# A graph network kernel: three count tables, searches in two steps, and the neighbour sums of both layers by seven block products

## The chip, the cores and the metric

The kernel runs on one core of a Trainium2 chip. The metric is the device time of one execution in microseconds (us), the median of three runs. A profiled execution gives a trace of every instruction; its span runs from the first instruction to the last, and the time of the run is a little longer than its span. The engines are PE (TensorE, matrix products), DVE (VectorE), ACT (ScalarE), POOL (GpSimd) and SP (SyncE, which here only issues transfers). Each of them works through its own list of instructions in order.

## What is computed

Two blocks follow one another on 384 nodes with 1024 features, in float32:

```
h = relu(layernorm(x));  x = x + L0(h)      # attention with an edge mask
h = relu(layernorm(x));  x = x + L1(h)      # relational graph convolutions

L0: q, k, v = h @ w.T + b, then q2, k2, v2 = (q, k, v) @ wi.T + bi      # 1024 x 1024 each
    mask[src, dst] = softplus(weight of the edge's type), the last edge of a cell wins
    out = softmax(q2 k2.T / 8 + mask) v2 @ wo.T + bo                    # 16 heads

L1: x = relu(h @ w_in + b_in)                                           # 1024 -> 768
    twice:
        counts[r, n] = edges of type r that end in node n
        agg[n] = sum over edges (r, src -> n) of (x @ W_r)[src] / counts[r, n]
        x = batchnorm(relu(agg + x @ root + bias) + x)                  # W_r = sum_b comp[r, b] basis[b]
    out = layernorm(x @ w_out + b_out)
```

There are 12672 edges, six edge types in L1 and four basis matrices.

## The kernel before

**Edges.** The kernel keeps no list of messages. It builds dense tables in device memory: four mask tables of 384 x 384 cells and two count tables of 384 x 6 x 384 cells (`mtab`, `atab`, lines 169 and 170). The edges come in 99 chunks of 128. For each chunk one indirect transfer of POOL writes mask values (`put_mask`, L261) and one adds counts (`put_count`, L266). [...]DVE first compares the edges of a chunk with each other (`find_cells`, L250): one comparison for the mask's cell, one for the mask's cell with the edge type. A piece has up to 12 chunks, so a search is a first half of 12 comparisons, preceded by a shift (`cells`, L241), and a second half of 12. Counts 0 to 10 go to table 0, the later ones to the two tables in turn. The first counts are interleaved with the mask puts; most of them follow after the last mask put. The tables are cleared beforehand by transfers of zeros on SP (`clear`, L271).

**The order of the edge work** is written out by hand. `edge_steps` is a generator with a body per step; the projections call `fill(1)` once per quarter of a weight matrix, which runs one step. Which step clears what, searches which piece and puts which rounds is listed there.

**Projections.** q2, k, k2 and v are computed by seven block products in place of eight (`multiply`, L377): DVE forms sums S of weight blocks (`output_sums`, L371) and sums T of input blocks (`node_sum`, L364), and adds parts of the result (L496, L502, L504).

**Attention** follows, then the output product (L615) and the input product of L1 (`ps_x`).

**The graph layers.** A relation's counts A[r] (128 partitions x 3 x 384) are loaded from both count tables: near the end of attention SP loads two relations from table 0 (L656), POOL loads the other four (L660) and adds table 1 to each (L658). `add_up` (L332, L333) sums A[r] over its three blocks on POOL; `share` sums that over the partitions by a matrix product with ones (`ps_cnt`, L338), takes the reciprocal on DVE (L340, L341) and has POOL scale A[r] (L342). `mix` combines the six scaled relations into four matrices At[b], one per basis matrix: r = 0 on ACT (L324), r = 1 to 5 on DVE (L326). The dictionary `between` names, by layer, basis and piece of it, after which products a share or a mix is emitted:

```python
        between = {(0, 1, 1): shares(0), (0, 1, 2): shares(1),
```

For each layer PE first computes H[b] = X basis[b] for four b (L846 and L840; again seven block products, with DVE sums L780, L787, L789, L795 and additions L853, L861, L863), then X root (L880), then adds the neighbours' sum, which is H[b] times At[b] over four b and three blocks of nodes. In layer 0 this is done directly: 72 products of 384 columns (L897). In layer 1 it is done in halves, with seven block products of 192 columns in place of eight (L947), sums of At (L953 to L957), sums of H (L969) and additions (L979) on DVE. After it each feature block is rectified, added to the layer's input and normalised (L902 to L918). Layer 1's matrices At are mixed anew during its products.

A float32 product appears in the trace as two matmul instructions.

Of the kernel before, what the change touches and what calls it, by code (L numbers as in the profile page):

```python
# [51 lines left out]
def gnn_kernel(ctx: ExitStack, tc: tile.TileContext, out, x, edges, chunks, cols, rows, small,  # L52
# [117 lines left out]
    atab = [tables.tile([ACELLS + P, 1], F32, name=f"atab{i}") for i in range(2)]  # L170
    keys_d = tables.tile([PAD, P], I32, name="keys_d")

    def edge_steps(ep, none, zero):
# [90 lines left out]
        def put_count():  # L264
            i, c = next(counts)
            nc.gpsimd.indirect_dma_start(atab[0 if i < 18 - DEALT else i % 2][:, :],  # L266
                                         bass.IndirectOffsetOnAxis(at[:, 1, c:c + 1], 0),
                                         count[:, 1, c:c + 1], None, compute_op=ALU.add)
# [20 lines left out]
        for find_more in rest:  # L289
            find_more()  # L290
        for step in range(2, 18):
            yield
            for i in {5: (0,), 6: (1,), 7: (2, 3), 8: (4, 5)}.get(step, (step - 4,) if 10 <= step < 16 else ()):
                clear(i // R, i % R)
            if step in (3, 6, 8, 10, 12, 14, 16):
                find_cells(max(3, step // 2 + 1))()
            for p in {8: (3,), 9: (4,), 10: (5,), 11: (6,), 16: (7, 8), 17: (9,)}.get(step, ()):
                put_rounds(p)
# [35 lines left out]

    def share(r):
# [6 lines left out]
        nc.gpsimd.tensor_tensor(A[:, r], A[:, r], rn[:, None, :].to_broadcast([P, NT, N]), ALU.mult)  # L342
        if r + 2 < R:
            add_up(r + 2)


    with ExitStack() as inner:
# [284 lines left out]
        for g in range(STEPS + 1):  # L632
# [14 lines left out]
            if f + 2 == STEPS:  # L647
# [7 lines left out]
                for r in range(2):  # L655
                    nc.sync.dma_start(A[:, r], tabs[0][r])  # L656
                for r in range(R):
                    nc.gpsimd.dma_start(A[:, r], tabs[1][r], accum_op=ALU.add)  # L658
                    if r + 2 < R:
                        nc.gpsimd.dma_start(A[:, r + 2], tabs[0][r + 2])  # L660
                    if 0 < r < 3:
                        add_up(r - 1)
# [103 lines left out]
    with tc.tile_pool(name="conv", bufs=1) as cp:  # L766
# [41 lines left out]
        def mixes(l, r, *bs):  # L808
            return lambda: mix(l, r, At, bs)

        between = {(0, 1, 1): shares(0), (0, 1, 2): shares(1),
                   (0, 2, 0): lambda: (mix(0, 0, At), share(2)), (0, 2, 1): mixes(0, 1, 0, 1), (0, 2, 2): mixes(0, 1, 2, 3),
                   (0, 2, 4): shares(3),
                   (0, 3, 0): mixes(0, 2, 0, 1), (0, 3, 1): lambda: (mix(0, 2, At, (2, 3)), share(4)),
                   (0, 3, 2): mixes(0, 3, 0, 1), (0, 3, 4): shares(5),
                   (0, 4, 0): mixes(0, 4, 0, 1), (0, 4, 1): mixes(0, 5, 0, 1), (0, 4, 2): mixes(0, 3, 2, 3),
                   (0, 4, 3): mixes(0, 4, 2, 3), (0, 4, 4): mixes(0, 5, 2, 3),
# [10 lines left out]
        for l in range(L):  # L828
# [49 lines left out]
            for k in range(KC):  # L878
                for o in range(KC):
                    nc.tensor.matmul(pr[o], w[k // 2][:, k % 2, o * P:(o + 1) * P], XT[:, k, :], start=(k == 0),  # L880
                                     stop=(k == KC - 1 and l == L - 1))
                if k == 0:
                    rest()
                go_between(l, B, k)
            if l + 1 < L:
                w = load_basis(l + 1, 0)
            else:

                room = late.tile([P, R * NT * N], F32, tag="A", name="room")
                rowsB = room[:, :3 * D].rearrange("p (j d) -> p j d", j=3)  # L890
                for j, r in enumerate((R_BOUT, R_LNG, R_LNB)):
                    nc.scalar.dma_start(rowsB[:, j, :], rows[r:r + 1, :].to_broadcast([P, D]))

            def add_neighbours(o, bs):
                for b in bs:
                    for n in range(NT):
                        nc.tensor.matmul(pr[o], H_[:, b, n, o * P:(o + 1) * P], At[:, b, n, :],  # L897
                                         start=False, stop=(b == B - 1 and n == NT - 1))
# [21 lines left out]
            def begin(o, func=AF.Identity):  # L920

                c = l * KC + o
                nc.scalar.activation(XN[:, o, :], pr[o], func, bias=cols_sb[:, CB + c:CB + c + 1])

            if l + 1 < L:
                for o in range(KC):
                    add_neighbours(o, (0, 1))
                for o in range(KC):
                    add_neighbours(o, (2, 3))
                    begin(o, AF.Relu)  # L930
                    normalise_layer(*measure(o))
                    if o == 2:
                        T = weight_sums(w)
            else:


                def h(o, i):

                    return H_.rearrange("p b n d -> p (b n) d")[:, i * 6:i * 6 + 6, o * P:(o + 1) * P]

                def q(i, j):

                    return At.rearrange("p b n d -> p (b n) d")[:, i * 6:i * 6 + 6, j * HN:(j + 1) * HN]

                def times(ps, x, y, start=False, stop=True):
                    for c in range(6):
                        nc.tensor.matmul(ps, x[:, c], y[:, c], start=start and c == 0, stop=stop and c == 5,  # L947
                                         skip_group_check=True)

                room2 = keep.tile([P, KD * N], F32, tag="hT", name="room2")  # L950
                T1, T2 = [room2[:, i * 1152:(i + 1) * 1152].rearrange("p (c d) -> p c d", c=6) for i in range(2)]
                T4 = keep.tile([P, 6, HN], F32, tag="mask8", name="T4")
                nc.vector.tensor_tensor(T1, q(0, 1), q(0, 0), ALU.subtract)  # L953
                nc.vector.tensor_tensor(T2, q(1, 1), T1, ALU.subtract)
                T3 = q(0, 1)
                nc.vector.tensor_tensor(T3, q(1, 1), q(0, 1), ALU.subtract)
                nc.vector.tensor_tensor(T4, q(1, 0), T2, ALU.subtract)  # L957
                spaces = [room2[:, 2304:]] + [room[:, 3 * D + i * 768:3 * D + (i + 1) * 768] for i in range(5)]
                spaces = [v.rearrange("p (c o) -> p c o", c=6) for v in spaces]

                def feature_sums(p):

                    s0, s1, s3 = spaces[p % 2 * 3:][:3]
                    o0, o1 = 2 * p, 2 * p + 1
                    S.append((s0, s1, h(o1, 0), s3))
                    for dst, x, y, op in ((s0, h(o1, 0), h(o1, 1), ALU.add), (s1, s0, h(o0, 0), ALU.subtract),
                                          (h(o1, 0), h(o0, 0), h(o1, 0), ALU.subtract),
                                          (s3, h(o0, 1), s1, ALU.subtract)):
                        nc.vector.tensor_tensor(dst, x, y, op)  # L969
                        yield  # L970

                S = []
                for _ in feature_sums(0):
                    pass
                pairs = KC // 2

                def take(o, j, ps):
                    dst = XN[:, o, j * HN:(j + 1) * HN]
                    nc.vector.tensor_tensor(dst, dst, ps, ALU.add)  # L979

                def rectify(o):
                    nc.scalar.activation(XN[:, o, :], XN[:, o, :], AF.Relu)
                    return o

                def first_of(p):
# [146 lines left out]
```

## Time and profile before

| | |
|---|---|
| median of three runs | 737.99 us (736.06 to 738.41) |
| profiled execution | 735.77 us, span 734.0 us |
| PE busy | 713.5 us, 97% of the span |
| DVE busy | 472.9 us, 64% |
| POOL busy | 323.3 us, 44% |
| ACT busy | 147.2 us, 20% |
| granted PE clock, mean | 0.996 of full |
| count puts, L266 | 99, 160.0 us busy, 1616 ns each |
| transfers A<-atab on POOL | 10 of 576 KB |

The page gives for each engine its busy time and share of the span. A row of a group reads: line, engine, operation, written<-read, shapes, number, then busy time, mean time of one, idle time of the engine before it and what ended that. A line of the waits view reads: engine, line that waited, what it waited for, us in total, times, longest. A line in order of time begins with its start and its length in us; in brackets stands the idle time before it and what released it. Matmuls overlap, so their pace is read from start to start.

### The profile page before, as it was taken

What the parts mean: (1) busy time and instruction counts of PE and PEld (TensorE: products, weight loads), DVE (VectorE), ACT (ScalarE), POOL (GpSimd) and SP (SyncE); (2) the same over time, 40 slices, a digit from 0 to 9 for tenths busy, and PEclk for the clock granted to TensorE, in tenths of its full rate; (3) what the DMA queues carried; (4) which work ended last, traced back from release to release, by engine and by line L of the source; (5) the groups of instructions that cost most, each with busy time, mean ns of one, the idle gap of its engine ahead of it and who ended that gap; (6) DMA issues with size and microseconds to landing.
All of it is one profiled execution on the core that took longest, in us unless ns stands there. A gap on an engine that the chain in (4) does not pass through costs nothing.

```text
span 734.0 us, 8299 instructions
## 1 busy us (share of the span) xinstructions
PE 713.5 (97%) x3024; PEld 496.8 (68%) x3024; DVE 472.9 (64%) x1228; ACT 147.2 (20%) x338; POOL 323.3 (44%) x242
## 2 busy tenths in 40 slices
PE   8999989999999999999999999899999999999995
PEld 8759989999964444445995555555555555579943
DVE  6895897877504499625424779990187676506756
ACT  3201111111111477510131131100013111001100
POOL 1456777788886788587784454310000000030000
PEclk9999999999999999999999999999999999999999
DMA  7797766743447322623527953321003123700001
GB/s 296 261 346 231 221 182 209 212 148 115 116 119 240 59 1 2 215 0 47 127 2 169 312 163 129 129 83 46 0 1 107 66 85 129 271 29 1 1 29 57
DMA packets 40533, 90.96 MB, mean 124 GB/s; under 512 B 19644, under 2 KB 27680, under 8 KB 36270
## 3 DMA queue, kind: packets, MB, share of 16 engines
q1 hardware_dynamic: 18478, 79.62, 30.9%
q0 software_dynamic: 21008, 8.42, 10.4%
q10 hardware_dynamic: 1008, 2.41, 0.9%
q8 instruction: 23, 0.38, 0.2%
q14 instruction: 16, 0.13, 0.1%
HBM read 79.27 MB, written 11.16 MB: 123 GB/s over the span
## 4 chain that ended last, share of the span: by engine, by line
PE 86%; DVE 11%; ACT 1%; issue 1%; DMA 1%; DVEq 0%; ACTq 0%
PE ps_g L846 13%; PE ps_g L840 10%; PE ps_c L897 6%; PE ps_c L880 6%; PE ps_q L395 6%; PE ps_v L524 6%; PE ps_k L377 6%; PE ps_c L947 6%; PE ps_v L377 5%; PE ps_y L615 5%; PE ps_f L1054 4%; DVE same L250 3%; PE ps_q L377 3%; PE ps_x L377 3%; PE ps_o L608 2%; PE ps_s L563 2%
## 5 line engine op out<-in xcount | busy, mean ns | idle before, releaser
L266 POOL DMA_INDIRECT atab<-count,at x99 | 160.0, 1616 | 50.6 <-DMA atab<-count,at 26.2
L261 POOL DMA_INDIRECT mtab<-m_val,at x99 | 104.1, 1052 | 57.0 <-issue 24.4
L1041 POOL TENSOR_TENSOR x_sb<-x_sb,room 128x1024 f32<-128x1024 f32 x3 | 7.0, 2347 | 158.1 <-DMA room<-in_rows 158.1
L326 DVE SCALAR_TENSOR_TENSOR At<-A,small_sb,At 128x1152 f32<-128x1152 f32 x40 | 62.9, 1635 | 0.0
L840 PE MATMUL ps_g<-T,S 128*128 128x384 f32 x144 | 49.1, 486 | 0.0
L846 PE MATMUL ps_g<-w_c,XT 128*128 128x384 f32 x144 | 48.0, 487 | 0.0
L846 PE MATMUL ps_g<-w_c,XN 128*128 128x384 f32 x144 | 47.6, 486 | 0.0
L897 PE MATMUL ps_c<-At,H 128*128 128x384 f32 x144 | 46.6, 486 | 0.0
L395 PE MATMUL ps_q<-hT,w_q 128*128 128x384 f32 (+1 forms) x160 | 41.8, 422 | 1.4 <-ACT hT L90 1.4
L524 PE MATMUL ps_v<-w_v,v 128*128 128x512 f32 x96 | 41.9, 594 | 0.0
L840 PEld LDWEIGHTS ps_g<-T,S 128*128 128x128 f32 x144 | 27.4, 190 | 19.1
L897 PEld LDWEIGHTS ps_c<-At,H 128*128 128x128 f32 x144 | 27.4, 190 | 19.1
L846 PEld LDWEIGHTS ps_g<-w_c,XN 128*128 128x128 f32 x144 | 27.4, 190 | 19.1
L846 PEld LDWEIGHTS ps_g<-w_c,XT 128*128 128x128 f32 x144 | 27.2, 190 | 19.2 <-DVE H L861 0.6
L395 PEld LDWEIGHTS ps_q<-hT,w_q 128*128 128x128 f32 x160 | 28.5, 190 | 14.1 <-ACT hT L90 1.7
L377 PE MATMUL ps_k<-T,S 128*128 128x192 f32 x192 | 35.8, 330 | 0.0
L615 PE MATMUL ps_y<-w_o,attT 128*128 128x512 f32 x80 | 35.0, 595 | 0.0
L576 DVE CUSTOM_DVE_ANT_0 s<-ps_s,mask 128x384 f32<-128x384 f32 x48 | 24.5, 548 | 15.4 <-PE ps_s L563 15.4
L342 POOL TENSOR_TENSOR A<-A,rn 128x1152 f32<-128x1152 f32 x6 | 19.4, 3236 | 31.7 <-DVE rn L341 31.7
L524 PEld LDWEIGHTS ps_v<-w_v,v 128*128 128x128 f32 x96 | 18.0, 190 | 22.6 <-issue 22.6
L377 PEld LDWEIGHTS ps_k<-T,S 128*128 128x128 f32 x192 | 32.7, 194 | 0.0
L1054 PE MATMUL ps_f<-w_out,XN 128*128 128x512 f32 (+1 forms) x84 | 31.1, 531 | 0.0
(250 smaller groups left out, 1316.6 us busy)
## 6 DMA issues: line engine op xcount, KB each, us to landing
w_c<-in_basis SPq DMA_DIRECT2D x24, 768.0 KB, 6.2
atab<-zero SPq DMA_DIRECT2D x12, 576.0 KB, 8.2
A<-atab POOLq DMA_DIRECT2D x10, 576.0 KB, 9.8
w_c<-in_root SPq DMA_DIRECT2D x6, 768.0 KB, 5.5
w_q<-in_wq SPq DMA_DIRECT2D x4, 1024.0 KB, 11.8
w_q<-in_wiq SPq DMA_DIRECT2D x4, 1024.0 KB, 10.1
w_k<-in_wk SPq DMA_DIRECT2D x4, 1024.0 KB, 7.0
w_k<-in_wik SPq DMA_DIRECT2D x4, 1024.0 KB, 6.2
```

The lines of the kernel that those rows point to most:

```text
L261: nc.gpsimd.indirect_dma_start(mtab[c // PER][:, :], bass.IndirectOffsetOnAxis(at[:, 0, c:c + 1], 0), m_val[:, c:c + 1], None)
L266: nc.gpsimd.indirect_dma_start(atab[0 if i < 18 - DEALT else i % 2][:, :], bass.IndirectOffsetOnAxis(at[:, 1, c:c + 1], 0), count[:, 1, c: ...
L326: nc.vector.scalar_tensor_tensor(At[:, b], A[:, r], w, At[:, b], ALU.mult, ALU.add)
L377: nc.tensor.matmul(ps, a[:, k, :], b[:, k, :], start=start and k == 0, stop=(k == 3), skip_group_check=not start)
L395: nc.tensor.matmul(ps[o][:, c], wt_[:, k, o * P:(o + 1) * P], src[:, k, c], start=(k == 0 and c.start == 0), stop=(k == KD - 1 and c.stop ...
L524: nc.tensor.matmul(ps, v[:, k, t * P:(t + 1) * P], w[k // 4][:, k % 4, :], start=(k == 0), stop=(k == KD - 1))
L615: nc.tensor.matmul(ps, attT[:, k, t * P:(t + 1) * P], w_o[half][k // 4][:, k % 4, :], start=(k == 0), stop=(k == KD - 1))
L840: nc.tensor.matmul(ps, x[:, c], y(c), start=start and c == 0, stop=(c == 2), skip_group_check=not start)
L846: nc.tensor.matmul(ps, block(XT, n, i)[:, c], w[c][:, i, o * HC:(o + 1) * HC], start=(first and c == 0), stop=(c == 2 and (i == 1 or ps is ...
L880: nc.tensor.matmul(pr[o], w[k // 2][:, k % 2, o * P:(o + 1) * P], XT[:, k, :], start=(k == 0), stop=(k == KC - 1 and l == L - 1))
L897: nc.tensor.matmul(pr[o], H_[:, b, n, o * P:(o + 1) * P], At[:, b, n, :], start=False, stop=(b == B - 1 and n == NT - 1))
L1054: nc.tensor.matmul(p, XT[:, k, t * P:(t + 1) * P], w[k // 2][:, k % 2, c0:c1], start=(k == 0), stop=(k == KC - 1))
```

## The change

Five things change together.

1. A third count table. Counts from number 11 on (the first is 0) go to three tables in turn, the last six to tables 0 and 1. Each step from 10 to 15 clears two pieces in place of one.
2. Searches in two steps. The second half of a search is kept in `rest` and run at the beginning of the next step.
3. Filling A. SP loads all six relations from table 2; POOL adds tables 0 and 1 to each, in an order written out (`add_tables`), seven of the twelve before the first shares and five inside `share`.
4. Shares and mixes are emitted earlier: share 0 after the third piece of basis 0 of layer 0 (it was after the second piece of basis 1), and so on. All mixes of layer 0 are emitted by the second root piece.
5. Layer 0 computes its neighbour sum with the code of layer 1. The places for the sums of H are a part of `room2` and tiles S, w and T4. The weight sums for layer 1 (`weight_sums`), which stood after the third feature block, are emitted after the node sums at the end of layer 0.

```diff
-    atab = [tables.tile([ACELLS + P, 1], F32, name=f"atab{i}") for i in range(2)]
+    atab = [tables.tile([ACELLS + P, 1], F32, name=f"atab{i}") for i in range(3)]
...
-            nc.gpsimd.indirect_dma_start(atab[0 if i < 18 - DEALT else i % 2][:, :],
+
+            tab = atab[0 if i < 18 - DEALT else i % 3 if i < EC - 6 else i % 2]
+            nc.gpsimd.indirect_dma_start(tab[:, :],
...
+        rest = []
         for step in range(2, 18):
             yield
-            for i in {5: (0,), 6: (1,), 7: (2, 3), 8: (4, 5)}.get(step, (step - 4,) if 10 <= step < 16 else ()):
+            if rest:
+                rest.pop()()
+            for i in {5: (0,), 6: (1,), 7: (2, 3), 8: (4, 5)}.get(step, (step - 4, step + 2) if 10 <= step < 16 else ()):
                 clear(i // R, i % R)
             if step in (3, 6, 8, 10, 12, 14, 16):
-                find_cells(max(3, step // 2 + 1))()
+                rest.append(find_cells(max(3, step // 2 + 1)))
...
+    def add_tables(*rs):
+        for r, i in rs:
+            nc.gpsimd.dma_start(A[:, r], tabs[i][r], accum_op=ALU.add)
...
         nc.gpsimd.tensor_tensor(A[:, r], A[:, r], rn[:, None, :].to_broadcast([P, NT, N]), ALU.mult)
+        add_tables(*{0: ((3, 1), (4, 0)), 1: ((5, 0), (4, 1)), 2: ((5, 1),)}.get(r, ()))
         if r + 2 < R:
             add_up(r + 2)
...
-                for r in range(2):
-                    nc.sync.dma_start(A[:, r], tabs[0][r])
                 for r in range(R):
-                    nc.gpsimd.dma_start(A[:, r], tabs[1][r], accum_op=ALU.add)
-                    if r + 2 < R:
-                        nc.gpsimd.dma_start(A[:, r + 2], tabs[0][r + 2])
-                    if 0 < r < 3:
-                        add_up(r - 1)
+                    nc.sync.dma_start(A[:, r], tabs[2][r])
+                add_tables((0, 0), (1, 0), (0, 1), (2, 0), (1, 1))
+                add_up(0)
+                add_tables((3, 0), (2, 1))
+                add_up(1)
...
-        between = {(0, 1, 1): shares(0), (0, 1, 2): shares(1),
-                   (0, 2, 0): lambda: (mix(0, 0, At), share(2)), (0, 2, 1): mixes(0, 1, 0, 1), (0, 2, 2): mixes(0, 1, 2, 3),
-                   (0, 2, 4): shares(3),
-                   (0, 3, 0): mixes(0, 2, 0, 1), (0, 3, 1): lambda: (mix(0, 2, At, (2, 3)), share(4)),
-                   (0, 3, 2): mixes(0, 3, 0, 1), (0, 3, 4): shares(5),
-                   (0, 4, 0): mixes(0, 4, 0, 1), (0, 4, 1): mixes(0, 5, 0, 1), (0, 4, 2): mixes(0, 3, 2, 3),
-                   (0, 4, 3): mixes(0, 4, 2, 3), (0, 4, 4): mixes(0, 5, 2, 3),
+        between = {(0, 0, 2): shares(0), (0, 0, 4): shares(1),
+                   (0, 1, 0): lambda: mix(0, 0, At), (0, 1, 1): lambda: (share(2), mix(0, 1, At, (0, 1))),
+                   (0, 1, 2): mixes(0, 1, 2, 3), (0, 1, 4): shares(3),
+                   (0, 2, 0): mixes(0, 2, 0, 1), (0, 2, 1): mixes(0, 2, 2, 3), (0, 2, 2): shares(4),
+                   (0, 2, 4): lambda: (share(5), mix(0, 3, At, (0, 1))),
+                   (0, 3, 0): mixes(0, 3, 2, 3), (0, 3, 1): mixes(0, 4, 0, 1), (0, 3, 2): mixes(0, 4, 2, 3),
+                   (0, 3, 4): mixes(0, 5, 0, 1), (0, 4, 1): mixes(0, 5, 2, 3),
...
+            room2 = keep.tile([P, KD * N], F32, tag="hT", name="room2")
+            spaces = [room2[:, 2304:]]
             if l + 1 < L:
+                spaces += [v.rearrange("p i k o -> p (i k o)")[:, i * 768:(i + 1) * 768] for v, n in
+                           ((cp.tile([P, 4, 3, P], F32, tag="S", name="sums"), 2),
+                            (wpool.tile([P, 2, 6, P], F32, tag="w", name="sums"), 2)) for i in range(n)]
+                spaces.append(cp.tile([P, 3, HC], F32, tag="T4", name="sums").rearrange("p c d -> p (c d)")[:, :768])
                 w = load_basis(l + 1, 0)
...
-            if l + 1 < L:
-                for o in range(KC):
-                    add_neighbours(o, (0, 1))
-                for o in range(KC):
-                    add_neighbours(o, (2, 3))
-                    begin(o, AF.Relu)
-                    normalise_layer(*measure(o))
-                    if o == 2:
-                        T = weight_sums(w)
-            else:
...
             XT = XN
             if l + 1 < L:
                 S = node_sums(XT)
+                T = weight_sums(w)
```

## The prediction

> **What bounds the kernel now.** I read first the busy shares: TensorE (PE) works 713.5 of 734.0 us, so time can only go where PE stands still or where it gets fewer products. Then PE's waits (engine and line, what it waited for, us in total, times, longest), with the Pool engine's wait of interest from the same view:
>
> ```profile
> PE 713.5 (97%) x3024; PEld 496.8 (68%) x3024; DVE 472.9 (64%) x1228; ACT 147.2 (20%) x338; POOL 323.3 (44%) x242
> ```
>
> ```profile
> PE ps_k L377 <- DVE k L502: 4.3, 3, 2.9
> PE ps_c L880 <- DVE H L853: 2.2, 1, 2.2
> PE ps_v L377 <- DVE v L502: 1.1, 1, 1.1
> PE ps_q L377 <- DVE q L502: 0.3, 1, 0.3
> POOL atab L266 <- DMA atab<-count,at: 26.2, 19, 4.3
> ```
>
> Three of the four PE waits are one thing: in the projections PE waits for VectorE's addition L502, queued behind a search. PE's order in time (start, length) shows that such a stop costs more than its wait:
>
> ```profile
> 101.48 1.46 PE L377 MATMUL ps_k<-T,S 128*128 128x192 f32 x8
> 105.86 2.61 PE L377 MATMUL ps_k<-T,w_k 128*128 128x192 f32 x8 [2.92 <-DVE k L502]
> 108.26 2.14 PE L377 MATMUL ps_k<-T,S 128*128 128x192 f32 x8
> 110.24 1.46 PE L377 MATMUL ps_k<-hT,w_k 128*128 128x192 f32 x8
> ```
>
> Eight matmuls take 1.30 us start to start, but the first sixteen after this stop take 2.40 and 1.98. The chain that ended last gives the two neighbour sums, old form and new (the second layer has the new one already):
>
> ```profile
> 499.77 46.44 PE ps_c L897 x144
> ...
> 654.57 40.95 PE ps_c L947 x252
> ```
>
> Last, the Pool engine around the end of the counts, in order of time:
>
> ```profile
> 385.05 1.55 POOL L266 DMA_INDIRECT atab<-count,at  x1 [0.30 <-issue]
> 392.67 1.36 POOL L658 DMA_DIRECT2D A<-atab  x1 [6.07 <-DVE T L795]
> ...
> 399.05 1.00 POOL L332 TENSOR_TENSOR sum<-A 128x384 f32<-128x384 f32 x1 [2.15 <-DMA A<-atab]
> 400.13 1.00 POOL L333 TENSOR_TENSOR sum<-sum,A 128x384 f32<-128x384 f32 x1
> ```
>
> The last count is issued by 386.6, the sums of relation 0 are ready at 401.1, and PE asks for them at 413.55 (its first ps_cnt matmul). That margin of 12.4 us is what the change spends.
>
> **What the skill says.** The Trainium skill, "TensorE: Matmul & The Clock Gate", Part 1, "What's actually happening": after an idle window of about 3.4 us PE falls to half clock until it has been busy about as long. The trace agrees: 3.1 us idle before 105.86, then 1.1 and 0.7 us lost, and a granted clock of 0.90 in 99 to 108 us. "DMA: Bandwidth & Descriptors", "Rules for kernel authors": an accumulating DMA must wait for the earlier DMA on the same bytes. Here both the puts into one table and the additions into one relation of A are such chains; a put lands 3.1 us (median, after 220 us) from its issue. "SBUF — State Buffer", "SBUF: two separate sides": Pool and a VectorE operation with two SBUF inputs exclude each other. The trace agrees: a mix (L326) takes 1.41 us, but four at 439.06 take 9.16 while Pool scales and sums.
>
> **The change part by part**, against the profiled span 734.0.
>
> *Neighbour sums of layer 0.* 72 products of 384 columns (144 instructions, 46.44 us) become 126 of 192 columns (252 instructions, 40.95): -5.49. VectorE gets four sums of At (1.27 each start to start) and four of H (0.87), 8.6 us, before the first product that needs them, 7.8 us into the stage (48 matmuls need none). By row durations I lay VectorE's queue from the start of the graph layers: the last mix ends 98 us in, these sums 106, the stage starts at 112, the need is at 120. So 14 us of slack; if mixes are so late that it is gone, each us costs one. At the end, weight sums of layer 1 (L787, L789: 3 x 1.47 = 4.4 us) move behind the last normalisation and the node sums. In the second layer the normalisation ends 4.8 us after the last product; 2.1 and 4.4 follow: 11.3. PE has 11.6 us of products that need none of it, and takes the last piece 1.3 us or more later still. Cost 0, hidden by those 36 matmuls.
>
> *Split searches.* A search is two halves, each 12 comparisons of 0.273 plus 0.3, and cells 0.95: 8.1 us at once, now 4.5 and 3.6 in successive steps of 9.1. In a step VectorE does sums S (2.6), search, then L496, L502, L504; L502 must be done 11.7 us after the step's start. Now: 0.3 + 2.6 + 8.1 + 0.6 = 11.6, over as soon as the 3.5 us of T sums join. After: 8.1. The five stops cost, by PE's starts against 1.30 per eight matmuls, 0.59 + 4.86 + 0.56 + 1.38 + 1.41 = 8.80. Most crowded after is the step of the 4.86: sums of T (1.8), S (2.5), half a search (4.5), T4 (0.87), L496, L502: end about 102.0 against a need at 102.8. So all 8.80 go; bounds 6 and 8.8. PE is then 8.8 early at the mask: it was ready at 232.6 and first used at 238.4, now wanted at 229.6. PE does 7 us of second-value products before it needs the result back, so up to about 2.6 us of delay of Pool is free.
>
> *Third table.* Puts wait for the put two before, now three before: 1.85 us more room. After 220 us there are 16 waits, 23.4 us, of which 0.30 each is the fixed gap: 18.6. Waits above 1.85 keep a rest, and around 300 to 312, where landings took 8.2 and 9.5, three waits keep all but one put's worth: 5.6 stay, 13 go (at most 16). Against it six more clears of 576 KB on SP between 87 and 137 us. They stand ahead of keys and weights on SP (0.43 each), which VectorE has room for, but puts land behind their data. Two steps that have two clears now cost Pool 4.7 us of extra waiting between 57 and 78, single ones about 0.45 each; so between 0 and 11 for six, I take 3. Last put issued by 386.6 - 13 + 3 = 376.6.
>
> *A is filled earlier and its shares move up.* SP loads all six relations from table 2 (done some 11 us before the last put; behind it on SP only weights that no free buffer admits before 400.84). Pool adds twelve transfers. Relation 0 needs two in a chain: first 1.6 after the last put (385.05 landed by 388.1), each 6.3 (fastest landing of L658) to 9.8 (median of Pool's A transfers); with six SP loads beside them I take 7.3. Then two sums, 2.0. Ready: 376.6 + 1.6 + 14.6 + 2.0 = 394.8. PE now asks at 384.69 + 11.61 - 8.80 = 387.5, in order, everything behind it waiting: a stop of 7.3, and 1.8 for the slow restart. Relation 1 follows about 5.5 us later, needed 8.4 later; those after have over 5 us.
>
> *Root matmuls.* They stand 2.38 us at 476 for L853, behind a mix. Mixes now spread from b = 1 on; laid out, L853's successor ends about as its bank is wanted: -2.4, bounds -2.4 and +2.
>
> Sum: PE leaves share 0 at 394.8 + 1.8 against 396.3 before, +0.3; then -5.49 and -2.38: 734.0 + 0.3 - 7.9 = 726.4. The profiled run took 735.77, 1.77 above its span, and the median shown is 2.22 above that: 730.4, so 730 us.
>
> **Rivals.** *Pool is in time:* puts end at 371 and two adds take 12.6, relation 0 ready at 387. No stop: 734.0 - 8.8 - 7.9 = 717.3, time 721. For it: SP's data land before the last put; against: the accumulating transfers kept the DMA engines 0.9 busy around 400.
> *Slower:* Pool as the bound. If the third table saves nothing, because puts land late for the DMA engines' sake and not for the table's, the last put ends at 389.6 with the clears: ready 407.8, span 739.4, 743 us. It decides from 404.6, that is from a last put at 386.4, where it is now. For it: 8.2 and 9.5 us landings at 300 to 312; against: 13 of the 16 waits are under 2.
> *The gain is just paid back:* ready between 400 and 404.6, 736 to 740 us; between these two.
> *The searches don't help*, L502 being late for the T sums: PE asks 3 us later, but Pool binds anyway, and the time stays 730. So this one is hidden.
>
> **How the numbers follow.** A measurement of this kernel tells about 0.3% (2.2 us) from no change. Chances: Pool late by 1 to 12 us 0.59 (723 to 735), in time 0.20, paid back 0.11, slower 0.10. Point 730; range 721 to 738: from the in-time case to the middle of the paid-back one. Faster 0.79, same 0.11, slower 0.10.
>
> **What would show it.** Right: no waits of PE on L502's successor; 252 neighbour matmuls in 41 us in layer 0; the last put near 377; one PE wait of 5 to 10 us on the first ps_cnt matmul, released by Pool's sum. Wrong: puts that end after 386; a PE wait on a mix or weight sum between 400 and 500 or after the neighbour sums; a stop at the mask near 235.

## The result

The changed kernel took 743.86 us (742.85 to 745.04), the kernel before 737.02 us on the same chip: ratio 1.0085, 95% interval 1.0061 to 1.0108. It is slower by 0.85%, where 730 us was forecast. The profiled execution has a span of 742.9 us against 734.0; it is the slowest of its four, and the profiled execution of the kernel before (735.77) was quicker than any of the four runs behind its 737.02, so the spans differ by 8.9 us and the medians by 6.8. Times and ratios are those of fast runs; one run of the late sites (748.3 us) and one of the moved clears (747.4), over 2% above the others of the same kernel, are left out.

The page's busy shares of the changed kernel, then the waits of PE and the one of POOL that answer to those shown of before (engine and line, what it waited for, us in total, times, longest):

```profile
PE 711.0 (96%) x3132; PEld 513.1 (69%) x3132; DVE 492.0 (66%) x1263; ACT 149.9 (20%) x344; POOL 323.5 (44%) x244
```

```profile
PE ps_cnt L347 <- POOL sum L338: 12.1, 1, 12.1
PE ps_g L854 <- DVE H L869: 4.0, 1, 4.0
PE ps_s L573 <- DVE top L586: 2.8, 1, 2.8
...
POOL atab L268 <- DMA atab<-count,at: 26.4, 14, 3.5
```

PE works 2.5 us less and the span is 8.9 us longer. All waits on the additions behind the searches are gone; three new ones stand in their place, and POOL waits for its counts as long as before (26.2 us then), in spite of the third table. In order of time PE passes the projections without a stop, and stops at the mask, at the first share and at a bank of H:

```profile
101.32 1.46 PE L387 MATMUL ps_k<-hT,w_k 128*128 128x192 f32 x8
102.62 1.47 PE L387 MATMUL ps_k<-T,S 128*128 128x192 f32 x8
103.92 1.47 PE L387 MATMUL ps_k<-T,w_k 128*128 128x192 f32 x8
...
241.75 3.40 PE L573 MATMUL ps_s<-k,q 64*128 64x384 f32 x8 [2.85 <-DVE top L586]
...
406.15 1.65 PE L347 MATMUL ps_cnt<-sum,ones 128*128 128x384 f32 x2 [12.12 <-POOL sum L338]
407.60 4.74 PE L848 MATMUL ps_g<-T,S 128*128 128x384 f32 x12
...
443.47 5.65 PE L854 MATMUL ps_g<-w_c,XT 128*128 128x384 f32 x12 [4.05 <-DVE H L869]
```

After each of these three stops the next matmuls are slow (3.40 us for eight, 1.56 without a stop; 4.74 and 5.65 for twelve, 4.03 without). The Trainium skill, "TensorE: Matmul & The Clock Gate", Part 1, "What's actually happening", puts this down to a clock that falls to half after an idle window of about 3.4 us. The trace agrees on the slow clock (0.69 granted in 404 to 412 us), not on the length: 2.85 us at the mask, 2.92 in the projections of the kernel before and 1.93 in a run below were enough, while after the 2.19 us at its root matmuls six of these took 2.14 us instead of 1.94. The chain that ended last shows why PE waited, and the two neighbour sums:

```profile
386.65 2.11 DMA atab<-count,at
388.76 1.65 issue
391.03 6.29 DMA A<-atab
397.83 6.14 DMA A<-atab
404.05 0.99 POOL sum L337
405.11 1.00 POOL sum L338
...
514.27 40.95 PE ps_c L946 x252
...
663.58 40.95 PE ps_c L946 x252
```

The last count's issue ends at 388.8, two additions of tables follow one another, and relation 0 is ready at 406.1; PE asked at 393.9. POOL's last counts in order of time (start, length, idle time before and its releaser):

```profile
375.70 1.55 POOL L268 DMA_INDIRECT atab<-count,at  x1 [0.63 <-DMA atab<-count,at]
380.70 1.55 POOL L268 DMA_INDIRECT atab<-count,at  x1 [3.45 <-DMA atab<-count,at]
382.56 1.55 POOL L268 DMA_INDIRECT atab<-count,at  x1 [0.31 <-issue]
386.65 2.11 POOL L268 DMA_INDIRECT atab<-count,at  x1 [2.54 <-DMA atab<-count,at]
```

Where the 8.9 us of span come from, by PE's starts against the kernel before:

| | us |
|---|---|
| start: the first sixteen projection matmuls in 4.49 instead of 2.84, and what precedes them | +1.7 |
| stops in the projections | -8.8 |
| mask: wait 2.85 and slow restart | +4.8 |
| share 0: wait 12.12 and slow restart | +13.8 |
| bank of H at 443: wait 4.05 and slow restart | +5.8 |
| root stall at 476 | -2.6 |
| neighbour sums of layer 0 | -5.5 |
| sum (measured: 8.9) | +9.2 |

### The profile page after: what moved, and what is told of

The parts are those of the page before. It is cut to its first block, busy times and chain, and to the rows that moved or that the text cites. A ratio compares the mean times of both kernels' runs of the same rounds, so it can differ in the third digit from the quotient of the medians.

```text
span 742.9 us, 8577 instructions
## 1 busy us (share of the span) xinstructions
PE 711.0 (96%) x3132; PEld 513.1 (69%) x3132; DVE 492.0 (66%) x1263; ACT 149.9 (20%) x344; POOL 323.5 (44%) x244
## 5 line engine op out<-in xcount | busy, mean ns | idle before, releaser
L261 POOL DMA_INDIRECT mtab<-m_val,at x99 | 102.6, 1036 | 57.0 <-issue 24.1
L976 DVE TENSOR_TENSOR XN<-XN,ps_c 128x192 f32<-128x192 f32 x38 | 12.6, 349 | 49.1 <-ACT XN L932 33.5
L405 PE MATMUL ps_q<-hT,w_q 128*128 128x384 f32 (+1 forms) x160 | 43.4, 436 | 1.4 <-ACT hT L90 1.4
L405 PEld LDWEIGHTS ps_q<-hT,w_q 128*128 128x128 f32 x160 | 30.2, 200 | 14.1 <-ACT hT L90 1.7
L946 PE MATMUL ps_c<-At,H 128*128 128x192 f32 x216 | 36.4, 326 | 0.0
L946 PEld LDWEIGHTS ps_c<-At,H 128*128 128x128 f32 x216 | 35.4, 190 | 0.5
L351 POOL TENSOR_TENSOR A<-A,rn 128x1152 f32<-128x1152 f32 x6 | 18.2, 3027 | 32.1 <-DVE rn L350 32.1
```

What stands on the lines that cost most here:

```text
L261: nc.gpsimd.indirect_dma_start(mtab[c // PER][:, :], bass.IndirectOffsetOnAxis(at[:, 0, c:c + 1], 0), m_val[:, c:c + 1], None)
L405: nc.tensor.matmul(ps[o][:, c], wt_[:, k, o * P:(o + 1) * P], src[:, k, c], start=(k == 0 and c.start == 0), stop=(k == KD - 1 and c.stop ...
```

## The experiments

Ratios are to the kernel before, run in turn on the same chip, with their 95% intervals; the times are medians. The runs of the kernel before spread from 733.7 to 743.1 us over the chips used, so a difference under some 0.4% is not told. Line numbers shift by a few between kernels.

### The kernel before, once more

> The kernel before, profiled once more. Theory: its first profile had a start that is not typical (the first sixteen projection matmuls in 2.84 us, where the changed kernel and four experiments took 4.3 to 4.5) and was spared a stop of PE on the H addition L861 near 455 that the experiments with the same work up to there showed at 4.7 us; at least the slow start shows again here, span 735 to 740. Rival: the first profile is typical (2.84 us, no stop at 455, span 734.0 within 1), and the edits cause both.

```profile
12.99 5.46 PE L395 MATMUL ps_q<-hT,w_q 128*128 128x192 f32 x16 [1.45 <-ACT hT L90]
```

Measured: span 735.3, time 737.1. The sixteen matmuls took 5.46 us with no edit at all, so the slow start is chance: over all profiles of this study it was 2.84 in four of sixteen and 4.3 to 5.5 in the others, with and without the edits in both groups. The 1.7 us of the table are therefore no effect of the change. The half about the stop near 455 was wrong: 0.17 us here. The last count's issue ended at 387.1 (386.6 in the first profile) and the first transfer of the mask tables' values began at 219.4 (218.4). These are the marks for the counts below, but they are loose: the seven-only run of the next section has the same edge work, and there the last count's issue ended at 391.6 and the mask's values were read from 219.9. One profile tells the last count to some 5 us only.

### The parts one by one

Split searches alone, seven products alone, and both (two tables and the old sites of the shares in all three):

```diff
+        rest = []
         for step in range(2, 18):
             yield
+            if rest:
+                rest.pop()()
...
-                find_cells(max(3, step // 2 + 1))()
+                rest.append(find_cells(max(3, step // 2 + 1)))
```

> The kernel before with the split searches alone (two tables, old sites, old sums of layer 0). Theory: the five stops of 8.8 us in the projections go, Pool delivers as before (mask ready at 232.6, relation 0 at 401.1), and PE asks 8.8 us earlier, for the mask at 229.6 with about 2.6 us free and for share 0 at 404.7, after it is ready: span 734.0 - 8.4 to 8.8 = about 725.4, ratio 0.988. Rival (Pool binds whatever PE does): a PE stop of 3 to 5 us with its slow restart shows at the mask or at share 0, ratio 0.994 to 1.0.

> The kernel before with the seven products in layer 0 alone. Theory: the neighbour sums go from 46.4 to 41.0 us; the last mix ends at 495.7, the eight sums of At and H (8.6 us) at 504.3, against a need 7.8 us after 499.8, at 507.6, so nothing stops: ratio 0.9926 (731.5). Rival: with the mixes this late VectorE misses the need or layer 1 starts late for its weight sums: a PE stop of 2 to 5 us after the first 48 products or at the end of the layer, ratio 0.997 to 1.0.

> The kernel before with the split searches and the seven products of layer 0, two tables, old sites: the late-sites experiment without its third table. Theory: with two tables one late put after the mask (8.9 us in the split-only run) holds Pool, the last put ends near 392 and relation 0 is ready near 411, so PE stops at share 0 for 3 to 4 us, and the stop on H follows: the product of the two single experiments, 1.002 x 0.994 = 0.996 (0.991 to 1.000); the third table is then worth about 0.7% at these sites. Rival (the third table is worth nothing at late sites): 0.985 to 0.990 as in the late-sites run.

Measured: split searches 739.45 us, ratio 1.002 (0.9987 to 1.0052); seven products 732.81, 0.9939 (0.9913 to 0.9965); both 731.96, 0.9893 (0.9844 to 0.9942). The seven products bring about what they should (0.9926 was expected), although the profile of each of the three kernels has 4.7 us of a stop on H, of which the two profiles of the kernel before have at most 0.2. The split searches alone bring nothing that can be told, and my theory for them fell: POOL does not deliver as before. From POOL's order in time in that run:

```profile
233.82 1.56 POOL L266 DMA_INDIRECT atab<-count,at  x1 [8.92 <-DMA atab<-count,at]
...
408.89 0.99 POOL L335 TENSOR_TENSOR sum<-A 128x384 f32<-128x384 f32 x1 [6.77 <-DMA A<-atab]
```

One count waits 8.9 us just after the mask tables are read back; with the old searches the longest wait at this place was 2.9, 3.5 and 4.0 us in three profiles with two tables, with split searches and two tables 8.1 to 9.0 in five, with split searches and three tables 2.3 to 3.5. PE that is 7 us ahead also frees its weight buffers 7 us earlier (SP, which waits for PE before them, issues the first load of w_o at 202.6 instead of 210.0), so other transfers fall on the read-back. The mask itself, read as early as before (218.1), landed later: it was ready at 238.0 instead of 232.6, and PE waited 0.2 us for it.

The last count ends at 391.9, but that is no later than in the seven-only run (391.6), where relation 0 was ready at 406.0 and PE did not stop for it. What is longer is the way from the last count to relation 0, 19.0 us instead of 14.4: before its sum POOL waits 6.8 us for the transfer (second line) and not 2.15. Relation 0 is ready at 411.0, and PE stops there for 3.6 us and on H for 4.7. Over eight profiles with two tables this way took 14.4 or 14.5 us where SP issued the next weights of a basis at 400.8 or later (the kernel before twice, seven products alone, and the changed kernel on two tables below), and 18.3 to 19.0 where PE had let it issue them between 392.2 and 395.2, beside these transfers (split searches alone, both together, and the last two versions below). That the weights are the cause, here and at the read-back, is not shown: no run moves them alone.

For both together the forecast was the product of the single ratios, 0.996 (0.991 to 1.000). The 0.9893 lies in the range of the rival, by which the third table is worth nothing at these sites, and its interval meets both. The profiled execution of that kernel, its slowest of four, has stops of 3.3 us at share 0 and 4.7 on H.

### The third table

Alone on the kernel before, with its clears, its loads of A and its chain of two additions:

> The kernel before with the third table alone: its six clears, the puts over three tables, A loaded from table 2 and two chained additions; old searches, old sites, old sums. My prediction's step: 13 us of waits go, 3 come for the clears, the last put ends at 376.6. Working theory now: the clears cost Pool 5 us before the mask, the six loads of A 4 to 5 us before the last put, and the last put ends at 384 to 389, no earlier than before (386 to 387); relation 0 is ready at 402 to 406. PE asks for it at 413 to 415 in either case, so the time shows nothing: ratio 0.996 to 1.004.

```profile
374.85 1.55 POOL L268 DMA_INDIRECT atab<-count,at  x1 [2.22 <-DMA atab<-count,at]
378.00 1.55 POOL L268 DMA_INDIRECT atab<-count,at  x1 [1.60 <-DMA atab<-count,at]
381.33 1.55 POOL L268 DMA_INDIRECT atab<-count,at  x1 [1.78 <-DMA atab<-count,at]
383.18 1.55 POOL L268 DMA_INDIRECT atab<-count,at  x1 [0.30 <-issue]
```

Measured: 736.07 us, ratio 0.9987 (0.9969 to 1.0005), no difference, as the working theory had it. The last count's issue ended at 384.7, relation 0 was ready at 402.9. Against the three profiles with old searches and two tables the last count gains 1.9, 2.4 and 6.8 us, and not 10. The waits of the counts, each less the fixed 0.30, show where:

| | third table alone | two tables (three profiles) |
|---|---|---|
| mask values read from | 223.3 | 218.4, 219.4, 219.9 |
| waits between 225 and 360 us | 6.4 | 16.8, 17.0, 20.0 |
| waits after 360 us | 5.6 | 1.9, 1.7, 1.7 |

So the six clears cost about 4 us before the mask, the third table saves 10.4 to 13.6 us in the middle, and about 4 us are lost again at the end, beside the six loads of A that SP issues from 370.2 on (4.7 in the rows shown). Its way from the last count to relation 0, with two additions in a chain, took 18.2 us.

The changed kernel back on two tables:

```diff
-                for r in range(R):
-                    nc.sync.dma_start(A[:, r], tabs[2][r])
...
+                for r in range(2):
+                    nc.sync.dma_start(A[:, r], tabs[0][r])
+                for r in range(R):
+                    nc.gpsimd.dma_start(A[:, r], tabs[1][r], accum_op=ALU.add)
...
```

> The changed kernel with two tables, without the six extra clears, and with the loading of A and the additions of the kernel before (one chained addition per relation); searches split, shares at the new sites, seven products. Theory: without the clears the mask stop of 4.8 us goes; relation 0 is ready at 401 to 402 instead of 406.1, and PE, asking near 389, still stops some 13 us; the stop at 443 stays: about 5 us faster than the changed kernel, 737 to 741 us, ratio 1.000 to 1.005. Rival (the third table is worth its cost): relation 0 is later than 406, ratio 1.010 or more.

Measured: 747.47 us, ratio 1.0139 (1.0112 to 1.0165). The rival's ratio came. The mask stop goes, as it should without the clears, but the last count ends at 391.7, relation 0 is ready at 406.1 all the same, and relation 2 stops PE once more (3.7 us at 431.8). So with these sites the third table is worth 0.5%, by what follows relation 0 and not by relation 0. At the old sites, where both versions have split searches and seven products, it is worth nothing that can be told: 0.9888 with it (next section), 0.9893 without.

### The sites of the shares

The changed kernel with the dictionary `between` of the kernel before, then with its own dictionary one site later:

```diff
-        between = {(0, 0, 2): shares(0), (0, 0, 4): shares(1),
+        between = {(0, 1, 1): shares(0), (0, 1, 2): shares(1),
...
```

```diff
-        between = {(0, 0, 2): shares(0), (0, 0, 4): shares(1),
-                   (0, 1, 0): lambda: mix(0, 0, At), (0, 1, 1): lambda: (share(2), mix(0, 1, At, (0, 1))),
+        between = {(0, 0, 4): shares(0), (0, 1, 0): shares(1),
+                   (0, 1, 1): lambda: mix(0, 0, At), (0, 1, 2): lambda: (share(2), mix(0, 1, At, (0, 1))),
...
```

> The changed kernel with shares and mixes back at the sites of the kernel before; three tables, split searches and seven products stay. Theory: share 0 is asked at about 410 instead of 394, after relation 0 is ready (406.1), so the 12.1 us stop with its restart goes, the stop at 443 too, the root stall of 2.4 us comes back, the mask stop of 4.8 us stays: span 742.9 - 13.7 - 5.7 + 2.4 = 725.9, time 727 to 729, ratio 0.987 to 0.990. Rival: relations 1 to 5 are later than their sites too, or the late mixes lay VectorE behind the need of the seven products: ratio 0.995 to 1.005.

> The changed kernel with its whole order of shares and mixes one site later, nothing else (share 0 after the last product of basis 0 instead of before, and so on). Theory (the sites are too early for what Pool delivers): PE asks for relation 0 near 401.6 instead of 393.9, Pool is ready at 405 to 406 as before, so the stop falls by about 7.7 us to 4 to 5; VectorE's queue behind it is served later by PE and its stop at 443 or 465 shrinks from 5.7 us to 0 to 3: 744 - 7.7 - 3 to 6 = 730 to 734, ratio 0.990 to 0.996. Rival (VectorE and Pool are full whatever the site, and only give the stop another place): above 1.000.

The waits of PE in the late-sites run, above 0.8 us:

```profile
PE ps_s L573 <- DVE top L586: 3.0, 1, 3.0
PE ps_c L888 <- DVE H L861: 2.0, 1, 2.0
...
PE ps_cnt L347 <- POOL sum L338: 0.9, 1, 0.9
```

(Waits of 1.1 to 1.4 us at the start and in attention, which all kernels have, are left out.) Measured: late sites 728.89 us, ratio 0.9888 (0.9849 to 0.9928), as the theory said. Against the changed kernel's 1.0085 the sites alone are worth 2.0%. One site later: 739.53, ratio 1.0015 (0.9993 to 1.0036), above the 0.990 to 0.996 of the theory. In its profile PE asked 6.0 us later (399.9; the site is 7.7 us later, and this profile's start was 1.6 us quicker) and the wait at share 0 fell by 6.0 us, from 12.1 to 6.1; but waits on H of 0.9 and 2.3 us stay, the second followed by a restart (5.82 us for twelve instead of 4.03). The part of the loss that is asking too early follows the site one to one; VectorE's part doesn't.

### VectorE's queue behind the shares

In the changed kernel four mixes stand in VectorE's queue before the additions to H for which PE waits until 443.47:

```profile
432.47 10.02 DVE L331 SCALAR_TENSOR_TENSOR At<-A,small_sb,At 128x1152 f32<-128x1152 f32 x4
442.42 0.54 DVE L861 TENSOR_TENSOR H<-H,ps_g 128x384 f32<-128x384 f32 x1
442.88 0.54 DVE L869 TENSOR_TENSOR H<-H,ps_g 128x384 f32<-128x384 f32 x1
```

The changed kernel with two mixes moved behind the H additions of their basis:

```diff
-                   (0, 1, 2): mixes(0, 1, 2, 3), (0, 1, 4): shares(3),
+                   (0, 1, 4): lambda: (share(3), mix(0, 1, At, (2, 3))),
```

> The changed kernel with one pair of mixes of relation 1 (b 2 and 3) moved behind the H additions of basis 1, nothing else. Theory: the 4.0 us stop of PE at 443 with its restart (5.7) comes of four mixes, 10.0 us while Pool scales and sums, queued before the H additions; with two of them the H additions are done before PE asks: stop gone, 738 us, ratio 1.0085 - 0.0075 = 1.001 (0.998 to 1.004). Rival (the bank is late for another reason, or the mixes only push the stop on): 1.006 to 1.010.

```profile
464.77 7.12 PE L854 MATMUL ps_g<-w_c,XT 128*128 128x384 f32 x12 [2.91 <-DVE H L869]
```

Measured: 742.95 us, ratio 1.0086 (1.0057 to 1.0114): no gain, the rival won. The stop at 443 is gone and one of about the same cost stands a basis later. In this run VectorE is not idle once from 416 to 465 us: reciprocals of 2.55, mixes of 2.5 us where POOL scales and sums beside them (1.4 without POOL), and weight sums. What is taken from in front of one addition stands in front of the next. The Trainium skill, "SBUF — State Buffer", "SBUF: two separate sides", describes an exclusive lock between POOL and a VectorE operation with two SBUF inputs. The trace agrees: in the changed kernel four mixes at 432.5 took 10.0 us while POOL worked, and four at 490.8, beside no work of POOL, 5.4.

### The clears

On the late-sites kernel, which still has the mask stop:

```diff
-            ... 8: (4, 5)}.get(step, (step - 4, step + 2) if 10 <= step < 16 else ()):
+            ... 8: (4, 5), 16: (12, 13), 17: (14, 15)}.get(step, (step - 4,) if 10 <= step < 16 else ()):
...
+        clear(2, 4)
+        clear(2, 5)
         for i in range(EC - PER + DEALT):
...
-            tab = atab[0 if i < 18 - DEALT else i % 3 if i < EC - 6 else i % 2]
+            tab = atab[0 if i < 18 - DEALT else i % 2 if i < 22 or i >= EC - 6 else i % 3]
```

> The late-sites experiment, with the clears of table 2 taken from between 87 and 137 us to behind 140 us, and table 2 used only from the 23rd count on (after the mask). Theory: the extra clears delay the mask puts by 5 us; without them the mask is read back near 219, and the 3.0 us stop at the mask with its restart (4.8 us) goes: 0.9888 - 0.0065 = 0.982 (0.979 to 0.985). Rival: the moved clears delay the mask puts just as much where they are now, or the mask is late for another reason: the stop stays, 0.986 to 0.992.

Measured: 729.13 us, ratio 0.9851 (0.9791 to 0.9911), which tells nothing by itself; the profile does. The mask values are read from 227.8, still later than with the clears at their old place (224.4), and PE's stop is 4.2 us. POOL lost less between 95 and 160, and lost it again at the two clears issued at 197: waits of 3.0 us at 206 and 2.3 at 226. The rival won: where the clears stand beside puts, the puts wait. A third placement is in the next section but one.

### The loads of A

The changed kernel with only relations 0 and 1 loaded by SP:

```diff
-                for r in range(R):
+                for r in range(2):
                     nc.sync.dma_start(A[:, r], tabs[2][r])
-                add_tables((0, 0), (1, 0), (0, 1), (2, 0), (1, 1))
+                add_tables((0, 0), (1, 0), (0, 1), (1, 1))
                 add_up(0)
-                add_tables((3, 0), (2, 1))
+                for r in range(2, R):
+                    nc.gpsimd.dma_start(A[:, r], tabs[2][r])
                 add_up(1)
+                add_tables((2, 0), (3, 0), (2, 1))
```

> The changed kernel with SP loading relations 0 and 1 only from table 2; relations 2 to 5 are loaded on Pool's queue behind the additions of relations 0 and 1. Theory: the six loads beside the last six puts are what holds these (waits 0.6, 3.5 and 2.5 us); with two loads the last put ends near 383 instead of 388.8 and the first ps_cnt wait falls from 12.1 to 6 to 8 us: 738 to 740 us, ratio 1.001 to 1.004, unless relation 2, added later now, stops PE near 426. Rival (two tables for the last six are what holds them): the waits stay, the first ps_cnt wait is 11 to 13, ratio 1.007 to 1.012.

```profile
380.93 1.55 POOL L268 DMA_INDIRECT atab<-count,at  x1 [0.30 <-issue]
```

```profile
399.62 1.65 PE L347 MATMUL ps_cnt<-sum,ones 128*128 128x384 f32 x2 [5.66 <-POOL sum L338]
...
425.37 1.65 PE L347 MATMUL ps_cnt<-sum,ones 128*128 128x384 f32 x2 [5.09 <-POOL sum L338]
```

The last count's issue (first fence) ends at 382.5 and none of the last three waits; 1.6 us of the 6.3 gained are this profile's quick start (the mask values are read from 222.8 instead of 224.4). Of the other 4.7, 3.8 are the four loads: after 360 us the counts wait 1.9 us above the fixed gap, and 5.6 to 5.9 in the seven profiles that have six loads. One of these, the one-site-later run, started as quickly as this one and waited 5.7. PE's wait at share 0 (second fence) falls from 12.1 to 5.7, and relation 2, now later, stops PE for 5.1. Measured: 744.03 us, ratio 1.0069 (1.0051 to 1.0087). The mechanism is as the theory had it, the gain is paid back at relation 2.

### Versions that beat both

Three tables, late sites, all extra clears at steps 15 to 17, and two pairs of mixes behind the H additions; the same on two tables; and that with shares 0 and 1 one site later:

```diff
-                   (0, 2, 0): lambda: (mix(0, 0, At), share(2)), (0, 2, 1): mixes(0, 1, 0, 1), (0, 2, 2): mixes(0, 1, 2, 3),
-                   (0, 2, 4): shares(3),
+                   (0, 2, 0): lambda: (mix(0, 0, At), share(2)), (0, 2, 1): mixes(0, 1, 0, 1),
+                   (0, 2, 4): lambda: (share(3), mix(0, 1, At, (2, 3))),
...
-                   (0, 3, 2): mixes(0, 3, 0, 1), (0, 3, 4): shares(5),
+                   (0, 3, 4): lambda: (share(5), mix(0, 3, At, (0, 1))),
```

The clears of the first, and the shares of the last:

```diff
-            ... 8: (4, 5)}.get(step, (step - 4, step + 2) if 10 <= step < 16 else ()):
+            ... 8: (4, 5), 15: (11, 12), 16: (13, 14), 17: (15, 16, 17)}.get(step, (step - 4,) if 10 <= step < 16 else ()):
...
-        between = {(0, 1, 1): shares(0), (0, 1, 2): shares(1),
+        between = {(0, 1, 2): shares(0), (0, 1, 4): shares(1),
```

> The late-sites experiment with two edits: the six clears of table 2 at steps 15 to 17 (about 132 to 152 us, none later; table 2 used from the 23rd count on), and two pairs of mixes moved behind the H additions of their basis (relation 1, b 2 and 3; relation 3, b 0 and 1). Theory: four clears at 142 to 152 cost Pool under 2 us in the moved-clears run and the two at 197 cost 4 to 6, so without those the mask is read back near 220 to 221 and its stop of 3.0 us with restart (4.8) goes; the root stall of 2.0 to 2.4 goes with the mixes: 0.9888 - 0.0095 = 0.979 (0.976 to 0.983). Rival (the mask is late wherever the clears are): stop of 3 us or more at the mask, 0.985 to 0.989. Rival (VectorE has no slack for moved mixes): a stop after the first 48 products of the neighbour sums.

> The kernel before with split searches, seven products of layer 0 and the two pairs of mixes moved: two tables, no extra clears, one chained addition. Theory (the third table carries the late put after the mask): one wait of 8 to 9 us near 234 again, last put near 391, PE stop of 3 to 4 us at share 0; the stops on H and at the root go: 0.983 to 0.987, worse than the three-table version by 0.3 to 0.7%. Rival (the third table is worth nothing): within 0.2% of it, 0.977 to 0.981.

> The two-table version (split searches, seven products, two pairs of mixes moved) with shares 0 and 1 one site later than in the kernel before. Theory: its only stop behind the projections, 3.5 us at share 0 and some 2 us of slow restart, goes: 0.9858 - 0.005 to 0.007 = 0.979 to 0.981. Rival: VectorE gets the scales later and misses the need of the seven products or the H additions: 0.985 or more.

Measured: three tables 726.32 us, ratio 0.9862 (0.9830 to 0.9894); two tables 725.33, 0.9858 (0.9826 to 0.9890). Both beat the kernel before by 1.4%, and they can't be told apart: the third table is not needed. In the first the mask values are read from 222.5 and the stop is 1.9 us, so these clears cost less and not nothing, and the root stall is gone; the forecast of 0.979 was too good. In the second the late count (8.1 us) and a stop of 3.5 at share 0 are there, and no stop on H or at the root, as forecast; that it would be worse than the first by 0.3 to 0.7% fell.

Taking that last stop away made it worse, where 0.979 to 0.981 was forecast: 733.12 us, ratio 0.9934 (0.9911 to 0.9956). Share 0 no longer stops PE, but share 2 does, and for POOL, not for VectorE as the rival had it:

```profile
434.61 1.65 PE L341 MATMUL ps_cnt<-sum,ones 128*128 128x384 f32 x2 [9.60 <-POOL sum L336]
```

POOL's addition to relation 5 stood before the scaling and summing in its queue and waited 8.3 us for a transfer (3.1 in the version with the stop). By the view of transfers, those of A took 12.4 us (median) from issue to landing between 405 and 432, against 8.3 between 405 and 426 in the version with the stop, and the weights of a basis 11.7 against 8.7. SP issued these weights before 418.4, in the version with the stop only from 421.1 on: PE frees the buffers earlier, and the loads fall on the transfers of A. That this overlap is the cause wasn't tested apart.

## Why the prediction was wrong

*Neighbour sums of layer 0: right.* 252 matmuls in 40.95 us; the last sum for them ended at 505.0 against a need at 521.9, 17 us of slack where I had laid out 14; layer 1 begins at once at 555.05.

*Split searches: right on PE, wrong on what it sets free.* PE reached the second value product at 202.72 instead of 209.80, with a start 1.7 us later: 8.8 us. That the mask would tolerate it failed: its values were read 6.0 us later (1.2 of them were there at 95 us, before most of the clears) and the first of them landed in 8.0 us instead of 5.7, so it was ready at 240.9 instead of 232.6, and the stop cost 4.8. The 2.6 us that I had held to be free for POOL were not: in the split-only run the slow landing alone used them up. The sum didn't show this, since the wait at share 0 covers it; with late sites it is the largest stop left.

*Third table: the step that failed.* I had the last count at 376.6; it was 388.8. By the run with the third table alone the saving in the middle, 10.4 to 13.6 us, was near my 13, and the clears, about 4, near my 3. The term left out was the six loads of A. I noted that they are done before the last count and so cost the chain nothing, and did not count what they do to the last six counts, which have only two tables: about 4 us there, and 3.8 fewer in the run that moves four of them away. That explains 384.7. The other 4 us, from 384.7 to 388.8, stay open: among the six profiles with split searches, three tables and all six loads the changed kernel's is the latest (386.0 to 388.8), and the same edge work on two tables ended between 386.6 and 391.6.

*Chain to relation 0: right.* From the last count 18.2 us were forecast and 17.3 measured, and 18.2 with the third table alone. PE asked at 393.9 instead of 387.5, by the slow start and the mask.

*Root matmuls: the stall at 476 went, and a dearer one came.* I laid out L853's successor and not the additions of basis 1 (L869), whose bank PE wants after two shares: 5.8 us against bounds of -2.4 to +2.

So of the 16.5 us between 726.4 and 742.9, 11.3 are relation 0 being late (12.1 for the last count, less 0.9 for the chain), 5.8 the bank of H, and the rest -0.6. Three of the signs that I had named for being wrong came: counts that end after 386, a stop at the mask (at 241.8), and a PE wait behind the mixes. The rival "Pool as the bound" said last count 389.6, ready 407.8, time 743 us; measured 388.8, 406.1, 743.9. Its outcome was right and its reason was not: the third table does save, and the change gives it back with the clears, with the loads of A and in the 4 us that stay open. Its time is right partly by chance, since it too left out the 5.8 us.

I had treated the earlier sites as free as long as POOL came in time. They are what made the kernel slower: the same parts with the old sites take 728.9 us.

## To carry to other kernels

Moving a consumer earlier turns each later delay of its producer into a stop of the whole engine, so price the two together and give the site the slack of the worst delay seen, not of the mean. A resource that is bought to loosen one chain (here a third table) has to be filled and emptied by transfers of its own: count its clears and loads against every transfer they run beside (here about 4 us each), above all the last ones. An engine that runs ahead also asks for its next loads earlier, so look at what these will stand beside. And in a queue without a gap, moving work from in front of one deadline puts it in front of the next.

## What I had not expected

The first sixteen projection matmuls took 2.84 us in some executions and 4.3 to 5.5 in others, 2.84 and 5.46 with one and the same program; the Trainium skill, "TensorE: Matmul & The Clock Gate", Part 1, "What's actually happening", says that the clock's window runs freely and the start varies from run to run, and here that is 1.5 to 2.6 us, as much as several edits are worth. With two tables, a put into a count table just after 2.3 MB of read-back waited 2.9 to 4.0 us with the old searches and 8.1 to 9.0 with the split ones, where PE is 7 us further on. And taking a stop away can cost more than the stop: the version with 3.5 us of waiting at share 0 was 0.8% faster than the one without it.
